# Mixture-of-experts tokens: an indexed scatter into expert slots, with four tiles loaded at a time, in place of an indexed gather for each tile

## The chip, the cores and the metric

The kernel runs on one core of one Trainium2 chip. A time is the device time of one execution in microseconds (us). Engines are named as the profile names them: PE (TensorE matmul, with PEld for its weight loads), DVE (VectorE), ACT (ScalarE), POOL (GpSimd) and SP (SyncE, which here only issues transfers). A "q" behind a name (SPq) is the engine's sequencer, which issues transfers and waits.

## The reference

The input `x` is 8 sequences of 512 tokens with 128 features, all float32. Three blocks follow one another, each with a residual: a mixture of experts, a state-space block, and the same mixture of experts again with the same weights.

```python
x = x + 0.5 * ffn(layernorm(x))        # m = 0
x = x + attn(layernorm(x))             # "ssm" below; works on one sequence at a time
x = x + 0.5 * ffn(layernorm(x))        # m = 1

def ffn(x):                            # E = 12 experts, K = 3 per token, D = 128, H = 512
    topw, sel = top_k(x @ Wg, 3); topw = softmax(topw)
    y[e] = gelu(x @ Wup[e] + bup[e]) @ Wdown[e] + bdown[e]
    return sum over the 3 chosen experts of topw * y[e]

def attn(x):
    u = silu(x @ Wg + bg) * (x @ Wi + bi)
    y = Cp * (causal convolution of u with Bp * A**t) + Dp * u
    y = layernorm(y) * gamma + beta
    return (silu(y @ Wfg + bfg) * (y @ Wfu + bfu) @ Wfd + bfd) @ Wo + bo
```

## The kernel before, in words

**Groups, slots, tiles, quads.** The sequences form three groups, `GROUPS = [[0, 1, 2], [3, 4, 5], [6, 7]]`. A group has 12 chunks of 128 tokens (the last has 8), so 36 pairs of chunk and choice (the last has 24). `route(m, g)` normalises the group's tokens into `xn`, computes the logits, takes the top three experts and gives every pair of token and choice a slot, sorted by expert and padded to whole tiles of 128 slots. `posu` (L433) holds the slot of each pair, `etab` (L484) the expert of each tile. A group has 48 tiles (the last 36), and four tiles are a quad: 12, 12 and 9 quads a group, 66 quads in both layers. Below, m0g1 is group 1 in the first layer, m1g0 group 0 in the second, and sequences carry their numbers 0 to 7.

**From slots to tokens.** A tile needs the inverse: which token sits in each slot. L439 to L472 build it on DVE and PE. In batches of 12 pairs, two one-hot tensors `M` (L447, L453) and `L` (L458) are made on DVE and multiplied on PE (L467, 12 matmuls a batch) into `ix_ps`; L472 casts it to `slot`. `xn` is also stored to DRAM (`xn_d`, L305). Then each tile is fetched by one indirect DMA on POOL (L513, through `gather_next` at L681), which reads 128 rows of `xn_d` at the indices `slot[:, t]`.

**A quad on the engines.** `prepare` transposes its four tiles on PE (L715), copies them to `xT` on ACT (L717) and loads the experts' offsets. `stage` copies the expert's up weights to `wst` on DVE (L732, one copy a tile). `up` does the first matmuls (L739) and the Gelu on ACT (L743), `down` the second (L753). After the fourth tile DVE adds the bias into `ysb` (L764) and SP stores 256 KB to `y_d` (L765).

**Back to the tokens.** When a group's last quad is stored, `finish_group` starts a `combine` for each of its sequences. For each chunk it issues three indirect gathers on POOL from `y_d` at the slots `posu` (L513, through L547), and later adds the three rows with their weights to `X` on DVE (L534). In layer 0 the sequence then goes through `ssm_block`, and when a group's sequences are all done `route(1, g)` follows; in layer 1 the sequence is stored.

**The order of the work.** Each engine executes in the order in which Python emits the instructions (`manual_schedule`, L85). The main loop (L790 to L802) walks over the 264 tiles; `up` of tile t, `down` of tile t - 2 and the staging of tiles ahead are written in turn, and twice a tile `chains.tick()` advances the generators (routes, combines, ssm blocks) by one step of a clock that counts 1.05 us a tick. POOL has its own count, `pool["free"]`, of 1.25 us for each indirect DMA (`GATHER`), and an add is emitted 3 us (`LANDS`) after its gathers by that count. `gather_upto` fetches up to 12 tiles ahead (`AHEAD`); `need` ticks on, without tile work, while the next quad's route isn't done.

Of the kernel before, what the change touches and what calls it, by code (L numbers as in the profile page):

```python
# [9 lines left out]
F32 = mybir.dt.float32  # L10
F16 = mybir.dt.float16
I32 = mybir.dt.int32
U32 = mybir.dt.uint32
# [38 lines left out]
def kernel(ctx: ExitStack, tc: tile.TileContext, a: dict, out: bass.AP):  # L52
# [9 lines left out]

    nc = tc.nc
    x = a["L0_attn_x"]
    B, T, D = x.shape
    E, _, H = a["L0_ffn_Wup"].shape
    P = 128
# [12 lines left out]
    LANDS = 3.0  # L82
    assert D == P and T == 512 and sorted(sum(GROUPS, [])) == list(range(B))

    ctx.enter_context(tc.manual_schedule())  # L85
    const = ctx.enter_context(tc.tile_pool(name="const", bufs=1))
    rt = ctx.enter_context(tc.tile_pool(name="rt", bufs=1))
    res_p = ctx.enter_context(tc.tile_pool(name="res", bufs=G + 1))
# [1 line left out]
    work = ctx.enter_context(tc.tile_pool(name="work", bufs=2))  # L90
    mo = ctx.enter_context(tc.tile_pool(name="mo", bufs=3))
    dr = ctx.enter_context(tc.tile_pool(name="dr", bufs=G + 1, space=DRAM))
    ps_up = ctx.enter_context(tc.tile_pool(name="ps_up", bufs=2, space=PSUM))
    ps_t = ctx.enter_context(tc.tile_pool(name="ps_t", bufs=1, space=PSUM))
    ps_y = ctx.enter_context(tc.tile_pool(name="ps_y", bufs=2, space=PSUM))
# [4 lines left out]
    def side_psum(shape, name):  # L100
        return ps_s.tile(shape, F32, tag="side", name=name)
# [56 lines left out]
        nc.sync.dma_start(w[n], a[f"L0_attn_{n}"])  # L158
    bo_bc = const.tile([P, D], F32, name="bo_bc")
    nc.sync.dma_start(bo_bc, a["L0_attn_bo"].unsqueeze(0).to_broadcast([P, D]))  # L160

    ones = const.tile([P, P], F16, name="ones")
    nc.vector.memset(ones, 1.0)
# [102 lines left out]
    def route(m, g, first=False):  # L266
# [5 lines left out]
        NTP = NQS[g] * 4  # L272
        chunks = [X[c][:, i, :] for c in seqs for i in range(CS)]
        r, nmr = yield from ln_stats(chunks, 1e-5, f"m{j}")
        xn = rt.tile([P, NCM, D], F32, tag="xn", name=f"xn{j}")
        xn_d = dr.tile([NC * P, D], F32, tag=f"xn_d{NC}", name=f"xn_d{j}")
        lg_ps = None
        pts: dict = {}
        xnTs: dict = {}
# [18 lines left out]
        for s in range(n):  # L298
            for i in range(CS):
                norm(  # L300
                    xn[:, s * CS + i, :], chunks[s * CS + i], r, nmr, s * CS + i,
                    not first or i % 2 == 1,
                )
            eng = nc.scalar if first else nc.sync
            eng.dma_start(  # L305
                xn_d[s * T : (s + 1) * T, :].rearrange("(p n) d -> p n d", p=P),
                xn[:, s * CS : (s + 1) * CS, :],
            )
            yield 2
        lg_ps = side_psum([P, NC, E], f"lg_ps{j}")  # L310
        for s in range(n + 1):
# [123 lines left out]
            posu.rearrange("p k c -> p (k c)"), lane, 4.0, row, op0=ALU.mult, op1=ALU.add  # L435
        )
        yield

        ix_ps = side_psum([P, NTP], f"ix_ps{j}")  # L439
        tok = mid("tok", lambda c, t: (K, c))  # L440
        nc.vector.tensor_copy(tok, tokid[:, :, :NC])
        tok = tok.rearrange("p k c -> p (k c)")
        NB_ = 12
        for b in range(NCK // NB_):
            sl = slice(b * NB_, (b + 1) * NB_)
            M = mid("M", lambda c, t: (NB_, t), F16, 2)
            nc.vector.tensor_tensor(  # L447
                M,
                iota_t[:, :NTP].unsqueeze(1).to_broadcast([P, NB_, NTP]),
                tl[:, sl].unsqueeze(2).to_broadcast([P, NB_, NTP]),  # L450
                ALU.is_equal,
            )
            nc.vector.tensor_mul(  # L453
                M, M, tok[:, sl].unsqueeze(2).to_broadcast([P, NB_, NTP])
            )
            yield
            L = rt.tile([P, NB_, P], F16, tag="L", name=f"L{j}_{b}", bufs=2)
            nc.vector.tensor_tensor(  # L458
                L,
                iota_l.unsqueeze(1).to_broadcast([P, NB_, P]),  # L460
                lane[:, sl].unsqueeze(2).to_broadcast([P, NB_, P]),
                ALU.is_equal,
            )
            yield 2
            for i in range(NB_):
                n_ = b * NB_ + i
                nc.tensor.matmul(  # L467
                    ix_ps, L[:, i, :], M[:, i, :], start=n_ == 0, stop=n_ == NCK - 1
                )
            yield  # L470
        slot = res_p.tile([P, NTP], U32, tag=f"slot{NTP}", name=f"slot{j}")
        nc.vector.tensor_copy(slot, ix_ps)  # L472

        after = mid("after", lambda c, t: (t, E))
        nc.vector.tensor_tensor(
# [6 lines left out]
        nc.vector.tensor_reduce(et, after, AX.X, ALU.add)  # L482
        etab = res_p.tile([P, NTP], I32, tag=f"etab{NTP}", name=f"etab{j}")
        nc.vector.tensor_scalar(etab, et, float(E - 1), float(WW), op0=ALU.min, op1=ALU.mult)  # L484
        y_d = dr.tile([NTP * P, D], F32, tag=f"y_d{NTP}", name=f"y_d{j}")
        cw = res_p.tile([P, K, NC], F32, tag=f"cw{NC}", name=f"cw{j}")
        res[(m, g)] = (xn_d, slot, etab, posu, cw, y_d)
        yield

        den = mid("den", lambda c, t: (K, c))  # L490
# [18 lines left out]

    pool = {"free": 0.0}  # L510

    def indirect(dst, src, idx):
        nc.gpsimd.indirect_dma_start(  # L513
            out=dst,
            out_offset=None,
            in_=src[:, :],
            in_offset=bass.IndirectOffsetOnAxis(ap=idx, axis=0),
        )
        pool["free"] = max(pool["free"], chains.now) + GATHER
        return pool["free"] + LANDS  # L520

    def combine(m, g, s, after=None):

        _, _, _, posu, cw, y_d = res[(m, g)]
        xs = X[GROUPS[g][s]]
        yg = work.tile([P, CS, K, D], F32, tag="yg", name=f"yg{m}{g}{s}", bufs=2)
        lands = []
        done = 0

        def add():  # L530
            nonlocal done
            c = s * CS + done
            for k in range(K):
                nc.vector.scalar_tensor_tensor(  # L534
                    xs[:, done, :], yg[:, done, k, :], cw[:, k, c : c + 1], xs[:, done, :],
                    op0=ALU.mult, op1=ALU.add,
                )
            done += 1

        for i in range(CS):  # L540
            for k in range(K):
                while pool["free"] > chains.now + 3 * GATHER:
                    yield
                    if done < len(lands) and lands[done] <= chains.now:
                        add()
                c = s * CS + i
                t = indirect(yg[:, i, k, :], y_d, posu[:, k, c : c + 1])  # L547
            lands.append(t)
            yield
        if after is not None:  # L550
            after()
        while done < CS:
            if lands[done] <= chains.now:
                add()
            yield
# [123 lines left out]
    state = {"gathered": 0}  # L679

    def gather_next():  # L681
        n = state["gathered"]
        p, t = tiles[n]
        m, g = phases[p]
        q = n // 4
        if n % 4 == 0:
            xg[q] = mo.tile([P, 4, D], F32, tag="xg", name=f"xg{q}", bufs=AHEAD // 4 + 1)
        xn_d, slot = res[(m, g)][:2]
        indirect(xg[q][:, n % 4, :], xn_d, slot[:, t : t + 1])
        state["gathered"] += 1  # L690

    def gather_upto(n, most):
        for _ in range(most):
            if state["gathered"] < min(n, len(tiles)) and phases[tiles[state["gathered"]][0]] in res:
                gather_next()

    def need(n):

# [6 lines left out]
    def prepare(q):  # L705

        if q >= len(quads):
            return
        need(q * 4 + 3)
        p, lq = quads[q]  # L710
        etab = res[phases[p]][2]
        pt = ps_t.tile([P, 4, P], F32, tag="t", name=f"t{q}")
        src = xg.pop(q)
        for i in range(4):
            nc.tensor.transpose(pt[:, i, :], src[:, i, :], ident)  # L715
        xT = mo.tile([P, 4, P], F32, tag="xT", name=f"xT{q}", bufs=2)
        nc.scalar.copy(xT, pt)  # L717
        xgT[q] = xT
        _, vals = nc.values_load_multi_w_load_instructions(
            etab[0:1, lq * 4 : lq * 4 + 4],  # L720
            engines=[mybir.EngineType.PE, mybir.EngineType.DVE],
            min_val=0,
            max_val=(E - 1) * WW,
            skip_runtime_bounds_check_because="min(expert, E - 1) * WW by construction",
        )
        off[q] = vals
        wst[q] = mo.tile([P, 4, WS], F32, tag="wst", name=f"wst{q}", bufs=2)
# [20 lines left out]
    def down(t, h):  # L748
        q, i = divmod(t, 4)
        if i == 0:  # L750
            y_ps[q] = ps_y.tile([P, 4, D], F32, tag="y", name=f"y{q}")
        for k in range(KH):
            nc.tensor.matmul(  # L753
                y_ps[q][:, i, :],
                h[:, k, :],
                W[:, bass.ds(off[q][i] + (WS + k * D), D)],
                start=k == 0,
                stop=k == KH - 1,
            )
        if i == 3:  # L760
            p, lq = quads[q]
            y_d = res[phases[p]][5]
            ysb = mo.tile([P, 4, D], F32, tag="ysb", name=f"ysb{q}", bufs=2)
            nc.vector.tensor_tensor(ysb, y_ps.pop(q), wst[q][:, :, H + KH : WS], ALU.add)  # L764
            nc.sync.dma_start(  # L765
                y_d[lq * 4 * P : (lq + 1) * 4 * P, :].rearrange("(p n) d -> p n d", p=P), ysb
            )
            if lq == NQS[phases[p][1]] - 1:
                finish_group(*phases[p])
# [65 lines left out]
```

## Time and profile before

| | |
|---|---|
| median of 3 runs | 801.06 us (799.05 to 802.33) |
| the profiled execution's own time | 801.01 us |
| its span, first to last instruction | 799.2 us (1.8 us lie around it) |
| busy in the span | PE 624.4, PEld 585.2, DVE 495.1, POOL 475.3, ACT 427.2 us |
| indirect DMAs on POOL | 264 for tiles (`xg`), 192 for results (`yg`) |
| moved by DMA | 64.23 MB, 80 GB/s on average |

A row of the profile's table of groups names the line, engine and operation, then `out<-in` with buffer numbers left out, then the count; behind the bar stand the busy time in us and the mean ns of one, and then the engine's idle time just before these instructions with what ended it. The first `xT` copy of a phase marks where its tiles begin: m0g0 at 67.2, m0g1 at 173.0, m0g2 at 285.8, m1g0 at 438.4, m1g1 at 565.4 and m1g2 at 673.8 us.

### The profile page before, as it was taken

To read this page: it belongs to the slowest core of one execution; us is meant where nothing else is said; L and a number is where in the kernel's file an instruction comes from. 1 tells how busy PE (TensorE), PEld (TensorE's weight loads), DVE (VectorE), ACT (ScalarE), POOL (GpSimd) and SP (SyncE) were. 2 spreads that over 40 slices of the span, in tenths; PEclk is the share of its full clock that TensorE was granted. 3 is DMA by queue.
4 is the path that set the end of the run, shared out by engine and by line. 5 is a ranking of instruction groups with operands and counts; after the bars stand their busy time and mean duration, and the time that the engine had idled before them with its cause. 6 is when DMAs were issued, how large, how long until landed. Compare 5 with 4: busy or idle time off the path is not lost.

```text
span 799.2 us, 16191 instructions
## 1 busy us (share of the span) xinstructions
PE 624.4 (78%) x5114; PEld 585.2 (73%) x5114; DVE 495.1 (62%) x1518; ACT 427.2 (53%) x1324; POOL 475.3 (59%) x479
## 2 busy tenths in 40 slices
PE   0416989999899999989334998889999989998500
PEld 0306988999888989878112998878989889998500
DVE  1486387445876666676897474987575874533422
ACT  0203854767477676767313685457677556665300
POOL 4007744435777777774003777745177777777775
PEclk9999998999999999999566999899999999999855
DMA  8801322312223322332000232322123233324322
GB/s 276 247 0 49 119 60 47 74 53 91 71 79 87 81 74 77 77 85 95 0 1 17 66 119 78 70 56 66 37 80 116 77 71 103 103 81 90 105 66 68
DMA packets 45016, 64.23 MB, mean 80 GB/s; under 512 B 9547, under 2 KB 26374, under 8 KB 44934
## 3 DMA queue, kind: packets, MB, share of 16 engines
q0 software_dynamic: 15552, 33.06, 17.6%
q1 hardware_dynamic: 28864, 29.31, 10.9%
q8 instruction: 45, 0.74, 0.4%
q10 hardware_dynamic: 518, 0.82, 0.3%
q14 instruction: 37, 0.30, 0.1%
HBM read 39.55 MB, written 23.59 MB: 79 GB/s over the span
## 4 chain that ended last, share of the span: by engine, by line
PE 44%; DVE 23%; POOL 12%; issue 10%; DMA 6%; ACT 3%; DVEq 0%; POOLq 0%; SPq 0%; ACTq 0%
PE y L753 17%; PE up L739 16%; POOL yg L513 8%; POOL xg L513 5%; DVE wst L732 3%; DVE L L458 3%; DMA xg<-xn_d,slot 3%; PE t L715 2%; DVE X L534 2%; DMA W<-in_L_ffn_Wdown_dram 2%; DVE ysb L764 1%; DMA yg<-y_d,posu 1%; PE lg_ps L293 1%; PE ing_ps L575 1%; PE fu_ps L583 1%
## 5 line engine op out<-in xcount | busy, mean ns | idle before, releaser
L513 POOL DMA_INDIRECT xg<-xn_d,slot x264 | 273.6, 1036 | 226.5 <-DVE slot L472 114.7
L743 ACT ACTIVATE h<-up,wst 128x128 f32<-128x128 f32 x1056 | 302.6, 372 | 176.9 <-ACT h L743 68.3
L739 PE MATMUL up<-xT,wst 128*128 128x128 f32 x2112 | 287.7, 280 | 1.2 <-ACT xT L717 0.7
L753 PE MATMUL y<-W,h 128*128 x2112 | 287.2, 280 | 0.0
L739 PEld LDWEIGHTS up<-xT,wst 128*128 128x128 f32 x2112 | 266.3, 197 | 9.9 <-issue 8.5
L753 PEld LDWEIGHTS y<-W,h 128*128 128x128 f32 x2112 | 264.5, 196 | 4.8 <-issue 4.8
L513 POOL DMA_INDIRECT yg<-y_d,posu x192 | 193.5, 1008 | 88.5 <-issue 82.7
L732 DVE COPY wst<-W 128x644 f32 x264 | 123.5, 508 | 7.8 <-DMA xg<-xn_d,slot 1.2
L764 DVE TENSOR_TENSOR ysb<-y,wst 128x512 f32<-128x512 f32 x66 | 45.5, 689 | 120.4 <-PE y L753 120.1
L534 DVE SCALAR_TENSOR_TENSOR X<-yg,cw,X 128x128 f32<-128x128 f32 x192 | 67.6, 352 | 64.9 <-DMA yg<-y_d,posu 61.7
L717 ACT COPY xT<-t 128x512 f32<-128x512 f32 x66 | 39.1, 593 | 55.1 <-PE t L715 49.9
L715 PE MATMUL t<-ident,xg 128*128 128x128 f32 x264 | 44.2, 286 | 14.8 <-DMA xg<-xn_d,slot 14.7
L715 PEld LDWEIGHTS t<-ident,xg 128*128 128x128 f32 x264 | 32.8, 147 | 18.3 <-DMA xg<-xn_d,slot 18.3
L467 PE MATMUL ix_ps<-M,L 128*128 128x48 f16 (+1 forms) x192 | 8.6, 194 | 37.7 <-DVE L L458 35.8
L467 PEld LDWEIGHTS <-L 128*128 128x128 f16 x192 | 7.3, 104 | 41.3 <-DVE L L458 39.9
L256 ACT ACTIVATE xn<-X,nmr_m,r_m 128x128 f32<-128x128 f32 x58 | 24.2, 501 | 24.0 <-DVE nmr_m L250 22.9
L458 DVE TENSOR_TENSOR L<-iota_l,lane 128x1536 f16<-128x1536 f16 x16 | 28.0, 1750 | 0.0
L256 ACT ACTIVATE xa<-X,nmr_a,r_a 128x128 f32<-128x128 f32 x32 | 13.2, 482 | 17.2 <-DVE nmr_a L250 17.2
L256 ACT ACTIVATE yn<-y_ps,nmr_b,r_b 128x128 f32<-128x128 f32 x32 | 12.1, 468 | 15.5 <-DVE nmr_b L250 15.5
L293 PEld LDWEIGHTS lg_ps<-wgate,xnT 128*128 128x128 f32 x128 | 17.9, 218 | 2.1 <-ACT xnT L288 2.1
L293 PE MATMUL lg_ps<-wgate,xnT 128*128 128x12 f32 x128 | 17.7, 271 | 1.8 <-ACT xnT L288 1.8
L370 PE MATMUL rk_ps<-mask,ones 128*128 128x144 f16 (+1 forms) x6 | 1.6, 263 | 21.8 <-DVE d L366 21.8
(161 smaller groups left out, 459.2 us busy)
## 6 DMA issues: line engine op xcount, KB each, us to landing
y_d<-ysb SPq DMA_DIRECT2D x66, 256.0 KB
xg<-xn_d,slot POOLq DMA_INDIRECT x264, 2.9
xn_d<-xn SPq DMA_DIRECT2D x13, 256.0 KB
W<-in_L_ffn_Wup_dram POOLq DMA_DIRECT2D x12, 256.0 KB, 7.1
W<-in_L_ffn_Wdown_dram SPq DMA_DIRECT2D x12, 256.0 KB
yg<-y_d,posu POOLq DMA_INDIRECT x192, 2.5
X<-in_L_attn_x_dram SPq DMA_DIRECT2D x8, 256.0 KB
out_dram<-X SPq DMA_DIRECT2D x8, 256.0 KB
```

What stands on the lines that cost most here:

```text
L256: nc.scalar.activation(dst, src, AF.Identity, scale=r[:, i : i + 1], bias=nmr[:, i : i + 1])
L293: nc.tensor.matmul(lg_ps[:, s * CS + i, :], xnT[:, i, :], wgate, start=True, stop=True)
L458: nc.vector.tensor_tensor(L, iota_l.unsqueeze(1).to_broadcast([P, NB_, P]), lane[:, sl].unsqueeze(2).to_broadcast([P, NB_, P]), ALU.is_equal,)
L513: nc.gpsimd.indirect_dma_start(out=dst, out_offset=None, in_=src[:, :], in_offset=bass.IndirectOffsetOnAxis(ap=idx, axis=0),)
L534: nc.vector.scalar_tensor_tensor(xs[:, done, :], yg[:, done, k, :], cw[:, k, c : c + 1], xs[:, done, :], op0=ALU.mult, op1=ALU.add,)
L715: nc.tensor.transpose(pt[:, i, :], src[:, i, :], ident)
L717: nc.scalar.copy(xT, pt)
L732: nc.vector.tensor_copy(wst[q][:, i, :], W[:, bass.ds(off[q][i], WS)])
L739: nc.tensor.matmul(pu[:, k, :], wst[q][:, i, ts(k, P)], xgT[q][:, i, :], start=True, stop=True)
L743: nc.scalar.activation(h[:, k, :], pu[:, k, :], AF.Gelu, bias=wst[q][:, i, H + k : H + k + 1])
L753: nc.tensor.matmul(y_ps[q][:, i, :], h[:, k, :], W[:, bass.ds(off[q][i] + (WS + k * D), D)], start=k == 0, stop=k == KH - 1,)
L764: nc.vector.tensor_tensor(ysb, y_ps.pop(q), wst[q][:, :, H + KH : WS], ALU.add)
```

## The change

For all groups but m0g0 (the first) the inverse index isn't built. Instead each of the 36 (or 24) pairs of chunk and choice is one indirect DMA on POOL that writes the 128 rows `xn[:, c, :]` to the slots `posu[:, k, c]` of a DRAM tensor `xs_d[g]`, which lies in slot order. A quad is then one plain 256 KB load that SP issues, and it waits for all of the group's scatters. The group counts as routed (`res`) only once its last scatter is emitted. Slots that no token fills are read too, so the three `xs_d` are set to zero at the start by three stores. `xn` gets two buffers, and `yg` becomes a tile per chunk, with six of them, where it was a tile per sequence, with two. POOL leaves the manual schedule: its order is the tile framework's own, bound by the dependencies of the data and by the "written order" links between neighbours; the built program shows scatters ahead of gathers that were written before them.

```diff
-    ctx.enter_context(tc.manual_schedule())
+    ctx.enter_context(tc.manual_schedule(engines={ET.PE, ET.DVE, ET.Activation, ET.SP}))
...
+    zero = work.tile([P, 4 * D], F32, tag="row", name="zero", bufs=4)
+    nc.vector.memset(zero, 0.0)
+    for g in range(G):
+        xs_d.append(dr1.tile([NQS[g] * 4 * P, D], F32, name=f"xs_d{g}"))
+        nc.sync.dma_start(
+            xs_d[g].rearrange("(q p n) d -> p q (n d)", p=P, n=4),
+            zero.unsqueeze(1).to_broadcast([P, NQS[g], 4 * D]),
+        )
...
-        xn = rt.tile([P, NCM, D], F32, tag="xn", name=f"xn{j}")
+        xn = rt.tile([P, NCM, D], F32, tag="xn", name=f"xn{j}", bufs=2)
...
-            eng = nc.scalar if first else nc.sync
-            eng.dma_start( xn_d ... xn ...)
+            if first:
+                nc.scalar.dma_start( xn_d ... xn ...)
...
+        if first:
             (the index build, L439 to L472, as before)
+            out_.update(xn_d=xn_d, slot=slot)
+        else:
+            chains.start(scatter(m, g, xn, posu, out_))
...
+    def queued(made):
+        ins = getattr(made, "ins", made)
+        if "last" in pool:
+            tc.add_manual_dep(ins, pool["last"].name, ORDER, reason="written order")
+        pool["last"] = ins
+        pool["free"] = max(pool["free"], chains.now) + GATHER
+        return ins
...
+    def scatter(m, g, xn, posu, out_):
+        made: list = []
+        for c in range(NCS[g]):
+            for k in range(K):
+                while pool["free"] > chains.now + 3 * GATHER:
+                    yield
+                ins = queued(
+                    nc.gpsimd.indirect_dma_start(
+                        out=xs_d[g][:, :],
+                        out_offset=bass.IndirectOffsetOnAxis(ap=posu[:, k, c : c + 1], axis=0),
+                        in_=xn[:, c, :],
+                        in_offset=None,
+                    )
+                )
+                for o in made:
+                    tc.declare_no_dep(ins, o, query=..., reason="pairs have different slots")
+                made.append(ins)
+        out_.update(scatters=made, ready=pool["free"] + LANDS)
+        res[(m, g)] = out_
+        yield
...
-        yg = work.tile([P, CS, K, D], F32, tag="yg", name=f"yg{m}{g}{s}", bufs=2)
+            yg.append(work.tile([P, K, D], F32, tag="yg", name=f"yg{m}{g}{s}_{i}", bufs=6))
...
     def gather_next():
...
+        if "slot" in r:
+            indirect(xg[q][:, n % 4, :], r["xn_d"], r["slot"][:, t : t + 1])
+            state["gathered"] += 1
+            return
+        made = nc.sync.dma_start(
+            xg[q], xs_d[g][t * P : (t + 4) * P, :].rearrange("(p n) d -> p n d", p=P)
+        )
+        for o in r["scatters"]:
+            tc.add_manual_dep(getattr(made, "ins", made), o.name, SYNC, reason="scattered rows")
+        state["gathered"] += 4
```

`gather_upto` also stops where a route's scatters have not landed by the count (`ready`).

## The prediction

> **What bounds the kernel now.** I read the windows view first, cut where each group's first `xT` copy stands. Columns: engine busy time (instructions), granted clock, DMA share, GB/s.
>
> ```profile
> core 0: us, PE busy (x) PEld busy (x) DVE busy (x) ACT busy (x) POOL busy (x), PEclk, DMA share, GB/s
> 173.00:285.80 112.80, 107.34 (x904) 101.62 (x903) 80.49 (x254) 76.07 (x239) 78.56 (x75) 0.98 0.28 77
> 285.80:366.80 81.00, 76.46 (x604) 69.98 (x603) 56.67 (x199) 57.65 (x176) 62.09 (x63) 0.98 0.31 83
> 366.80:438.40 71.60, 33.93 (x187) 22.07 (x187) 58.74 (x196) 23.63 (x56) 10.50 (x10) 0.69 0.06 20
> 438.40:565.40 127.00, 116.99 (x950) 111.30 (x951) 86.38 (x261) 77.32 (x242) 84.98 (x83) 0.93 0.27 73
> 754.10:799.20 45.10, 0.00 (x0) 0.00 (x0) 12.39 (x35) 0.00 (x0) 29.89 (x32) 0.50 0.25 72
> ```
>
> In the tile phases PE is busy 92 to 95% of the time, so they are PE-bound. Two stretches are not: the hand-over to layer 1 (366.8 to 438.4), where PE does 34 us of work in 72, and the tail after the last quad, where only POOL works. Then the groups of instructions and the waits:
>
> ```profile
> L513 POOL DMA_INDIRECT xg<-xn_d,slot x264 | 273.6, 1036 | 226.5 <-DVE slot L472 114.7
> L513 POOL DMA_INDIRECT yg<-y_d,posu x192 | 193.5, 1008 | 88.5 <-issue 82.7
> L458 DVE TENSOR_TENSOR L<-iota_l,lane 128x1536 f16<-128x1536 f16 x16 | 28.0, 1750 | 0.0
> L467 PE MATMUL ix_ps<-M,L 128*128 128x48 f16 (+1 forms) x192 | 8.6, 194 | 37.7 <-DVE L L458 35.8
> ```
>
> POOL waits long for `slot`, once for 58.7 us (the hand-over). The timeline gives the prices of a hand-over and of a bare quad:
>
> ```profile
> 180.10 0.69 DVE L764 TENSOR_TENSOR ysb<-y,wst 128x512 f32<-128x512 f32 x1 [0.38 <-PE y L753]
> 180.82 0.32 SPq L765 DMA_DIRECT2D y_d<-ysb  x1
> ...
> 184.68 0.95 POOL L513 DMA_INDIRECT yg<-y_d,posu  x1 [14.09 <-issue]
> 185.93 0.95 POOL L513 DMA_INDIRECT yg<-y_d,posu  x1 [0.30 <-issue]
> 658.66 0.59 ACT L717 COPY xT<-t 128x512 f32<-128x512 f32 x1
> 666.25 0.59 ACT L717 COPY xT<-t 128x512 f32<-128x512 f32 x1
> 673.83 0.59 ACT L717 COPY xT<-t 128x512 f32<-128x512 f32 x1
> ```
>
> A 256 KB store to DRAM is usable 3.9 us after its issue; back-to-back gathers start 1.25 us apart (0.95 busy, 0.30 issue), and with the slower ones among them I take 1.27; a quad with no side work takes 7.6 us. From the groups, an ssm block costs PE 9.2 us (transposes 10.7 + 5.4 + 10.1, matmuls 10.2 + 9.0 + 9.5 + 10.1 + 8.5, over 8).
>
> **What the Trainium skill says.** "DMA: Bandwidth & Descriptors", § SWDGE vs HWDGE vs iDMA: a DMA issued by GpSimd gets a pair of descriptors (read, write) per operation. A scatter of 128 rows then has as many as a gather, hence the same price; the trace has gathers only. Same page, § Anatomy of one DMA: most of about 2 us of fixed cost is the write receipt, heaviest when DRAM is written. Gathers land 2.4 to 5.3 us after issue here (median 2.9 for `xg`), into SBUF; for a scatter no row exists. "SBUF — State Buffer", § Who interferes with whom: GpSimd blocks while DVE runs a copy in a two-port mode. The trace agrees weakly: minimum 941 ns, mean 1036 for `xg`.
>
> **The change, part by part.**
>
> *Index build, five routes.* Removed: 13 of 16 batches, DVE 13 × (1.750 + 0.725 + 0.711) = 41 us and PE 156 × 0.045 = 7 us, 13 SP stores and 216 `xg` gathers (274 us of POOL). POOL and DVE are not the limit in the tile phases, so most of this is worth nothing by itself.
>
> *Added:* 156 scatters × 1.27 = 198 us of POOL, 54 SP loads, three zero stores of 33 × 256 KB = 8.65 MB. At the SP queue's rate (29.31 MB in 10.9% of 799.2 us, 336 GB/s) these take 26 us from 36 us on. The DMA engines are idle then until the first gathers at 59.6, so 1 us is charged (0 to 5).
>
> *m0g0 to m0g1: +16.* `posu` is ready at 117.4. In the built program 15 `xg` gathers and the 36 scatters then share POOL: 51 × 1.27 = 65 us, to 182.4. Landing 2.6 (between the medians of `yg`, 2.5, and `xg`, 2.9) and a load 3.9 bring the first `xT` to 189, where it was at 173. PE stands in order behind that transpose with half a quad and m0g1 queued, and the store of m0g0's last quad stands behind the load on SP; before, the gathers were 25 us ahead. Bounds +10 and +30 (scatter at 1.15 and 1.55).
>
> *m0g1: 112.8 becomes 134.* POOL no longer mixes `xg` with `yg`: the results of m0g0 come back in 36 gathers without `xg` between, so ssm 0 to 2 all fall in m0g1, where about 1.5 did: + 1.5 × 9.2 - 1 for the index matmuls = + 13. And the order costs a wait: in POOL's order 22 of m0g2's 24 scatters stand ahead of or among the gathers of sequence 2, while DVE's fixed order has their adds where the count put them. The add of the sequence's third chunk is reached about 64 us into the phase, its rows land at 12 + 24 × 1.25 + 19 scatters × 1.25 + 9 × 1.25 + 2.4, about 79. DVE is held 15 us; PE has staged weights for about 7 us of it. + 8. m0g2 begins at 323 (was 285.8).
>
> *m0g2 and the hand-over: 152.6 becomes 117.* Work: 9 × 7.6 = 68.4, ssm 3, 4 and half of 5 (2.45 × 9.2 = 22.5), route 6, some inefficiency 2: 99. Then the rest of ssm 5 runs alone, a chain of DVE, PE and ACT steps of 15 (bounds 15 and 30: in the crowded hand-over of before the last block took 30), and a wait for adds of 3 as above. POOL is done by then: 12 + 72 × 1.25 + 2.4 + 3.9 = 108. The 58.7 us wait for `slot` goes because the route runs under m0g2's tiles; what is late next is ssm 5. m1g0 begins at 440 (was 438.4), with a block and a half more done.
>
> *m1g0: 127 becomes 121.* 91.2 + two blocks 18.3 + routes 9.4 + a cool clock 2. The 36 scatters come after all `yg` here and end 15 us early. m1g1 begins at 561 (was 565.4).
>
> *m1g1: 108.4 becomes 110.* Bare 91.2 + 4. But 14 scatters stand ahead of the eighth chunk's gathers, and 8 ahead of the eleventh's. The eighth chunk's rows land at 12 + 31.5 + 17.5 + 2.4 = 63, the add is reached at 45: 18 us held, about 10 for PE; the eleventh adds some 5. m1g2 begins at 671.
>
> *m1g2 and tail: 125.4 becomes 116.* No `xg` on POOL: eight quads at 7.6 and 15 to the last `ysb` are 76 (was 80.3). The last 24 gathers no longer queue behind those of m1g1: 0.7 + 3.9 + 24 × 1.24 + the 5.8 from the last gather's end to the span's end give 40 (was 45.1).
>
> Sum of the span: 189 + 134 + 117 + 121 + 110 + 76 + 40 = 787; with the 1.8 us around it **789 us**. The profiled execution took 801.01, the median is 801.06, so no correction.
>
> **Rivals.**
> 1. *The scatter's price (slower).* Some 100 POOL operations stand in a row with the end (36 before m0g1, 19 and 22 before held adds in m0g1 and m1g1, 22 in m0g2). Each 0.1 us more per scatter costs about 10 us; from 1.39 on the gain is gone. At 1.6: 0.33 × 100 = 33, **822 us**. For it: receipts from DRAM, and that no row shows it. Against: equal descriptor counts.
> 2. *Held adds cost PE nothing (faster).* If staged weights and the scatters' placing cover them, 8 + 3 + 15 = 26 come off: **763 us**. Against: m1g1 is PE-bound and recovers nothing.
> 3. *Gains and waits cancel:* 801. A scatter price between 1.35 and 1.43 does it.
> 4. *The order isn't as built:* not likely, since the program's lists show 156 scatters and 54 loads.
>
> **How the numbers follow.** No change means within 0.5% (4 us), about what a measurement can tell. As worked out 0.43, rival 2 0.14, so faster 0.57; rival 3 0.12; rival 1 0.31. The range reaches from rival 2's end to rival 1's, 762 to 824; the likeliest case's own is 775 to 797.
>
> **What would show it.** First `xT` of m0g1 near 189 with POOL full before it; the hand-over's wait for `slot` gone; DVE waits `X<-yg` above the 61.7 us of before, in m0g1 and m1g1; a scatter row near 1.0 us; last `ysb` near 747 and 40 us behind it. It is wrong if scatters have a mean above 1.2, if m1g0 doesn't begin within 10 us of 440, or if PE is held before m1g2 for another reason.

## The result and the profile after

The changed kernel took 843.01 us (median of 4 runs, 837.93 to 845.45) against 800.63 for the kernel before: a ratio of 1.0521 (95% interval [1.0466, 1.0575]; brackets behind a ratio mean this below), slower by 42 us, where 789 us were predicted. Its profiled execution has a span of 836.2 us. The experiments ran on several chips, and three of them are slower for every kernel (before itself: 1028 to 1051 us), so the text gives ratios to the kernel before on the same chip, and compares lengths of phases only between chips on which that kernel takes 798 to 801.

The page's groups of the changed kernel (`xs_d` is the scatter):

```profile
L549 POOL DMA_INDIRECT yg<-y_d,posu x192 | 191.0, 995 | 285.3 <-DMA xg<-xs_d 174.3
L817 PE MATMUL up<-xT,wst 128*128 128x128 f32 x2112 | 293.7, 284 | 35.1 <-DVE wst L810 31.5
L566 POOL DMA_INDIRECT xs_d<-xn,posu x156 | 160.1, 1026 | 69.6 <-issue 37.8
L597 DVE SCALAR_TENSOR_TENSOR X<-yg,cw,X 128x128 f32<-128x128 f32 x192 | 67.4, 352 | 102.5 <-DMA yg<-y_d,posu 99.6
```

The wait for `slot` is gone and a scatter is priced like a gather (1026 and 995 ns). Two waits are new or larger: DVE's adds `X` wait 99.6 us for gathered rows, and PE's `up` waits 31.5 us for staged weights. In the kernel before, `up` waited 1.2 us in all, and the adds 61.7 for rows:

```profile
L534 DVE SCALAR_TENSOR_TENSOR X<-yg,cw,X 128x128 f32<-128x128 f32 x192 | 67.6, 352 | 64.9 <-DMA yg<-y_d,posu 61.7
```

The windows view, cut as before at each group's first `xT`, here m0g1, m0g2 with the hand-over, m1g0 and m1g1:

```profile
core 0: us, PE busy (x) PEld busy (x) DVE busy (x) ACT busy (x) POOL busy (x), PEclk, DMA share, GB/s
188.30:333.60 145.30, 124.30 (x928) 111.88 (x928) 91.31 (x320) 85.76 (x261) 61.77 (x60) 0.91 0.23 70
333.60:462.70 129.10, 104.09 (x736) 89.38 (x735) 88.29 (x304) 72.69 (x214) 73.42 (x72) 0.92 0.23 72
462.70:598.60 135.90, 119.74 (x936) 111.80 (x936) 88.46 (x309) 84.95 (x260) 61.38 (x60) 0.95 0.25 79
598.60:719.80 121.20, 95.46 (x821) 94.86 (x821) 51.15 (x141) 62.19 (x206) 59.48 (x60) 0.89 0.30 92
```

In the kernel before, m1g1 was the line

```profile
565.40:673.80 108.40, 102.70 (x897) 98.61 (x896) 72.39 (x224) 72.50 (x230) 74.38 (x72) 1.00 0.30 83
```

m0g2 with the hand-over is shorter, 129.1 us where it was 152.6, and PE is idle in it for 25.0 us where it was for 42.2. But m0g1, m1g0 and m1g1, in which PE was 92 to 95% busy, are longer, with PE 79 to 88% busy. In m1g1 the waits and the timelines of POOL, DVE and PE show where the time goes:

```profile
DVE X L597 <- DMA yg<-y_d,posu: 42.5, 17, 17.7
PE up L817 <- DVE wst L810: 25.0, 2, 15.2
```

```profile
655.77 0.96 POOL L566 DMA_INDIRECT xs_d<-xn,posu  x1 [0.30 <-issue]
657.03 0.98 POOL L549 DMA_INDIRECT yg<-y_d,posu  x1 [0.30 <-DMA xs_d<-xn,posu]
```

```profile
659.53 0.39 DVE L597 SCALAR_TENSOR_TENSOR X<-yg,cw,X 128x128 f32<-128x128 f32 x1 [17.67 <-DMA yg<-y_d,posu]
```

```profile
663.92 2.05 PE L817 MATMUL up<-xT,wst 128*128 128x128 f32 x8 [15.20 <-DVE wst L810]
```

The scatter at 655.77 is the last of 14 in a row that stand ahead of the gather at 657.03. The row of that gather lands at 659.5; until then DVE has stood in its fixed order for 17.67 us, with the copies of the next quad's weights behind the add, and PE stands for 15.20 behind those.

### The profile page after: what moved, and what is told of

The parts are those of the page before. It is cut to its first block, busy times and chain, and to the rows that moved or that the text cites. A ratio compares the mean times of both kernels' runs of the same rounds, so it can differ in the third digit from the quotient of the medians.

```text
span 836.2 us, 15919 instructions
## 1 busy us (share of the span) xinstructions
PE 627.1 (75%) x4958; PEld 586.1 (70%) x4958; DVE 452.0 (54%) x1470; ACT 425.5 (51%) x1324; POOL 407.9 (49%) x419
## 3 DMA queue, kind: packets, MB, share of 16 engines
q1 hardware_dynamic: 39040, 48.71, 17.6%
## 4 chain that ended last, share of the span: by engine, by line
PE 40%; DVE 21%; POOL 13%; issue 11%; DMA 10%; ACT 3%; SPq 1%; DVEq 0%; POOLq 0%; ACTq 0%
PE y L831 15%; PE up L817 15%; POOL yg L549 7%; POOL xs_d L566 5%; DMA yg<-y_d,posu 3%; DVE wst L810 3%; DMA xs_d<-xn,posu 2%; DVE X L597 2%; DMA W<-in_L_ffn_Wdown_dram 2%; PE t L793 2%; PE lg_ps L307 2%; DVE ysb L842 2%; DMA xg<-xn_d,slot 1%; POOL xg L549 1%; PE ing_ps L639 1%
## 5 line engine op out<-in xcount | busy, mean ns | idle before, releaser
L549 POOL DMA_INDIRECT yg<-y_d,posu x192 | 191.0, 995 | 285.3 <-DMA xg<-xs_d 174.3
L817 PE MATMUL up<-xT,wst 128*128 128x128 f32 x2112 | 293.7, 284 | 35.1 <-DVE wst L810 31.5
L817 PEld LDWEIGHTS up<-xT,wst 128*128 128x128 f32 x2112 | 271.5, 200 | 47.2 <-issue 41.2
L566 POOL DMA_INDIRECT xs_d<-xn,posu x156 | 160.1, 1026 | 69.6 <-issue 37.8
L597 DVE SCALAR_TENSOR_TENSOR X<-yg,cw,X 128x128 f32<-128x128 f32 x192 | 67.4, 352 | 102.5 <-DMA yg<-y_d,posu 99.6
L549 POOL DMA_INDIRECT xg<-xn_d,slot x48 | 48.7, 1014 | 61.9 <-DVE slot L490 47.6
L793 PE MATMUL t<-ident,xg 128*128 128x128 f32 x264 | 43.1, 282 | 31.5 <-DMA xg<-xs_d 20.1
L633 PE MATMUL yn_ps<-ident,yn 128*128 128x128 f32 x32 | 10.6, 359 | 15.4 <-ACT yn L270 14.9
L633 PE MATMUL xa_ps<-ident,xa 128*128 128x128 f32 x32 | 10.8, 366 | 11.5 <-ACT xa L270 10.8
L633 PEld LDWEIGHTS yn_ps<-ident,yn 128*128 128x128 f32 x32 | 4.7, 148 | 20.8 <-ACT yn L270 20.8
```

Source lines behind the costliest of these rows:

```text
L549: nc.gpsimd.indirect_dma_start(out=dst, out_offset=None, in_=src[:, :], in_offset=bass.IndirectOffsetOnAxis(ap=idx, axis=0),)
L566: nc.gpsimd.indirect_dma_start(out=xs_d[g][:, :], out_offset=bass.IndirectOffsetOnAxis(ap=posu[:, k, c : c + 1], axis=0), in_=xn[:, c, :], ...
L597: nc.vector.scalar_tensor_tensor(xs[:, done, :], yg[done][:, k, :], cw[:, k, c : c + 1], xs[:, done, :], op0=ALU.mult, op1=ALU.add,)
L817: nc.tensor.matmul(pu[:, k, :], wst[q][:, i, ts(k, P)], xgT[q][:, i, :], start=True, stop=True)
```

## Experiments

Two theories. **A:** the loss is POOL's order, in which scatters overtake gathers that were written before them, so adds are held. **B:** 156 scatters themselves cost too much, by POOL's time in series or by what they do to others.

### 1. The scatters in written order

```diff
+        if scattered and "gather" in pool and pool["gather"] is not pool["last"]:
+            tc.add_manual_dep(ins, pool["gather"].name, ORDER, reason="behind the gathers")
+        if not scattered:
+            pool["gather"] = ins
```

> The change with one more link: a scatter may not stand ahead of a gather that was written before it, so POOL runs xg, then all yg of a group, then the next group's scatters; nothing else differs. Theory A (scatters put ahead of the gathers hold the adds on DVE, and with them the weights of PE and the late steps of the ssm blocks): the long holds of X<-yg at 270 and 640 to 690 us vanish, the m1g1 phase falls from 121 to 95-100, m0g1 from 145 to 128-135, the hand-over phase from 129 to 120-125; device time near 803 (793 to 812). Theory B (a tile waits for a whole group's scatters, which is what costs): m0g1 still begins at 188, and the time falls by at most 10, to 833 or more.

> The change, with each scatter linked behind the last gather that was written before it, so that no scatter overtakes a yg gather and no add is held behind one. If the held adds carry most of the loss (my theory by the prediction: some 20 us), the ratio falls from 1.052 to 1.03 or less where the matmuls issue freely; if they are a symptom of POOL being full, 1.04 to 1.05. Twice before on chips with a lower granted clock it was 0.011 under the change.

> The change with its scatters in written order (behind the gathers written before them), again, as the control of the three runs beside it, whose POOL instructions stand in this order. Three times before: 1.064 to 1.072 of the kernel before.

Measured: on the three slower chips 1.0723 [1.0646, 1.08], 1.0681 [1.0609, 1.0753] and 1.0644 [1.0571, 1.0717]; on a chip where the kernel before takes 798.94, **1.0012 [1.0001, 1.0023]** (799.89 us). There POOL's order was the whole loss against the kernel before. The windows of that run, m0g1 to m1g1, and its wait for rows in m1g1:

```profile
188.10:321.20 133.10, 121.56 (x928) 109.91 (x928) 92.03 (x320) 85.90 (x260) 61.32 (x60) 0.96 0.25 77
321.20:450.40 129.20, 104.12 (x738) 89.41 (x737) 88.58 (x304) 72.75 (x215) 73.54 (x72) 0.92 0.23 72
450.40:586.10 135.70, 119.55 (x936) 111.64 (x935) 88.32 (x309) 84.91 (x260) 61.22 (x60) 0.95 0.25 79
586.10:681.30 95.20, 91.72 (x818) 90.94 (x817) 52.83 (x145) 62.18 (x206) 60.40 (x60) 1.00 0.38 117
```

```profile
DVE X L602 <- DMA yg<-y_d,posu: 15.0, 17, 1.8
```

Against the change, m0g1 is 12.2 us shorter and m1g1 26.0. No run of the change is on record for this chip; that its phases can be set beside these follows from the other phases, which agree within 0.3 us. PE's wait for staged weights in m1g1 falls from 25.0 us to 0.9. On the one slower chip that ran both orders (the 1.0681), the change took 1.0799: there undoing the order gave about 1%, and the intervals overlap. Part 4 comes back to those chips.

### 2. What the 156 scatters cost

On the same chip, three edits of the change itself. In the traces of d1 and d2 POOL's operations stand in the order of the run above, one for one, though without the added link:

```diff
 (d1: a gather of as many rows into an unread SBUF tile; SP loads zeros; xn has one buffer)
-                        out=xs_d[g][:, :],
-                        out_offset=bass.IndirectOffsetOnAxis(ap=posu[:, k, c : c + 1], axis=0),
-                        in_=xn[:, c, :],
+                        out=seen[:, (c * K + k) % NCM, :],
+                        in_=xs_d[g][:, :],
+                        in_offset=bass.IndirectOffsetOnAxis(ap=posu[:, k, c : c + 1], axis=0),
 (d2: a plain transfer to rows in a row)
+                    nc.gpsimd.dma_start(out=xs_d[g][n * P : (n + 1) * P, :], in_=xn[:, c, :])
 (d3: nothing issued; only the count goes on)
+                pool["free"] = max(pool["free"], chains.now) + GATHER
```

These expectations were written for a chip on which the written order takes 1.06 to 1.07. The runs fell on one on which it takes 1.0012, and are read against that.

> Each scatter replaced, in its place, by a gather of the same size: 128 rows of 512 B taken from the zeroed DRAM tensor at the same positions into an SBUF tile that nothing reads; the SP loads still wait for the whole group of them, and read zeros. POOL's instructions are as many and about as long (0.96 us). If it is POOL's time in series and the wait for the whole group, 1.06 to 1.07 as the control. If it is the scatter itself (rows written to DRAM in an order of their own, behind which others' transfers or instruction fetches stand), 1.01 to 1.03, with PE idle in some 20 to 30% of these windows as in the gathers' and not 65 to 70%.

> Each scatter replaced, in its place, by a POOL transfer without an index: the same 128 rows of 512 B written to 128 rows in a row of the same DRAM tensor (wrong slots). If writing 64 KB from POOL's software queue is what costs, 1.05 to 1.07; if the index and its descriptors cost, 1.01 or less.

> The scatters left out altogether; the written order's clock goes on as if they were there, and SP loads zeros. It is the floor of what all 156 scatters together cost: if they carry the whole loss and more, 0.93 to 0.97, as two thirds of them gave 1.01 to 1.02 against 1.07; if something else of the change costs too (SP's loads, the zeroing, the earlier ssm blocks), above 1.00.

Measured: gathers in the scatters' places 0.9999 [0.9984, 1.0014], plain writes 0.9747 [0.9715, 0.9779], none 0.9673 [0.9644, 0.9703]. POOL's groups of the first two:

```profile
L567 POOL DMA_INDIRECT seen<-xs_d,posu x156 | 155.9, 999 | 69.1 <-issue 46.3 <-DVE posu L448 13.7 <-DVE msum_a L247 8.5
```

```profile
L567 POOL DMA_DIRECT2D xs_d<-xn x156 | 86.5, 563 | 0.4 <-issue 0.4
```

So writing to DRAM by index costs the end no more than reading by index, and most of the cost is the index's time on POOL: 1.0 us busy and 0.3 of issue, against 0.56 and no gap for a plain write. (A plain write also doesn't wait for `posu`: the first starts at 102.0 instead of 115.7. That head start was not needed: m0g1 begins at 168.4, at 168.1 with no scatter at all, and 36 × 0.56 + 15 gathers × 1.27 = 39 us from 115.7 on would also have been in time, by an estimate from these prices.) All scatters together are worth 797.4 - 769.3 = 28 us of span. 20.0 of these lie ahead of m0g1, whose first quad waits for all 36 (188.1 against 168.1 without); most of the rest is 1.7 in m1g0, 3.0 in m1g1 and 2.6 in the tail. The floor of 0.967 is also the most that free scatters could bring in this kernel: 798.9 - 772.3 = 27 us. The windows without scatters, m0g1 to m1g0:

```profile
168.10:301.00 132.90, 121.60 (x929) 109.97 (x930) 93.72 (x327) 85.89 (x261) 37.66 (x36) 0.96 0.21 65
301.00:429.80 128.80, 104.17 (x736) 89.57 (x735) 87.33 (x304) 72.67 (x214) 35.87 (x36) 0.92 0.18 54
429.80:563.80 134.00, 118.74 (x937) 111.08 (x936) 87.85 (x309) 84.86 (x260) 23.30 (x24) 0.95 0.20 62
```

Lengths are as with scatters, within 1.7 us. PE is idle 11.3 + 24.6 + 15.3 = 51 us in them; in the kernel before it was 5.5 + 42.2 + 10.0 = 58 over the same three phases. The hole of the hand-over was for the most part not filled, it was spread: PE's waits in m0g2 here are `yn_ps` for ACT's `yn` (8.3 us), `xa_ps` (4.1), `y_ps` (3.9) and `rk_ps` (2.5), which are steps of the ssm blocks and the route.

Leaving out only the third choice's scatters (104 instead of 156, so a third of the slots stays zero), in the change's own order, on two slower chips:

```diff
-            for k in range(K):
+            for k in range(K - 1):
```

> The change with the third choice's scatters left out (104 scatters instead of 156; the slots of the third choice keep zeros, so that part of the result is left out), all else as it is. Theory P (POOL's time for scatters, some 100 operations in a row with the end): 33 to 42 us come off, near 805; m0g1 begins near 173. Theory A: more in the places where scatters stand ahead of gathers, m1g1 near 105 and m0g1 near 135, and the total near 800. If the loss lies elsewhere (work moved on PE, the loads on SP): m0g1 begins earlier and the rest of the phases stay, about 828.

> The change without the third choice's scatters (104 instead of 156; those slots keep zeros, which leaves that part of the result out). Theory P, some 100 POOL operations in a row with the end: 33 to 42 less than the change, near 805, m0g1 from 173. If the phases after m0g1's start stay as they are: 828. At the lower clock it was at 1.019 of before, against 1.072 for the written order with all scatters: there the scatters' number counted most.

Measured 1.0189 [1.0116, 1.0262] and 1.0099 [1.0059, 1.0138]. On the second of these chips the whole change is 1.0799: 75 us for 52 scatters, or 1.4 us each. There undoing the order of all of them gives about 14 us, and on the faster chip all 156 are worth 28. Part 4 takes that up.

### 3. The first hand-over without scatters

The index build and gathers for m0g1 as well as m0g0 (`by_gather = first or (m, g) in ((0, 1),)` in place of `first`), in the change's order and in written order:

> The change, but m0g1 too is fetched by the index build and a gather for each tile, as before; the other four groups are scattered. Theory B: m0g1 begins at 173 instead of 188, and about 15 us come off: 828. If the scatters' place ahead of the gathers also cost in m0g1 (theory A), xg and yg now share POOL there and the order is another one: up to 10 more come off or are lost, 818 to 838.

> Both of the former: written order on POOL and m0g1 by gathers. Theory A with B: the two gains add up, near 788 (778 to 800), below the kernel before. If the only cost was the wait for whole groups (B alone): 825. m0g1 begins at 173; POOL carries 36 xg, 36 yg and 24 scatters in m0g1, some 122 us at 1.27, so its ssm blocks come later and the hand-over may give back up to 10.

> Scatters in written order, and the second group (m0g1) by index build and gathers as the kernel before has it. On the chip where the written order alone took 1.001, the scatters' own cost of 28 us lay in the first hand-over for 20: m0g1's first tile waited for 36 scatters to end, 188.1 against 168.1 without them, and 173.0 with the kernel before's gathers. With gathers there it should start at 173 and all that follows keep its lengths (133, 129, 136, 95, 75, 41): 782 us, a ratio of 0.98. On a chip where engines' issue is slow beside POOL's runs it should repeat 1.06.

Measured on a slower chip 1.0668 [1.0606, 1.0729] and, with written order, 1.0624 [1.0562, 1.0687]; on a chip with the kernel before at 798.2, **1.005 [1.0034, 1.0066]**, not the 0.98 expected. The windows of that run, m0g1 and m0g2:

```profile
170.90:307.90 137.00, 117.16 (x912) 105.51 (x912) 96.47 (x334) 83.65 (x253) 92.64 (x92) 0.93 0.26 72
307.90:452.50 144.60, 114.84 (x753) 98.20 (x752) 90.72 (x320) 76.12 (x222) 73.12 (x72) 0.88 0.22 66
```

m0g1 does start at 170.9, 17 us earlier. But its tile gathers now share POOL with the 36 gathers of m0g0's results, which run from 182.3 to 271.2 instead of 203.3 to 250.3; the 24 scatters of m0g2 end at 302.6 instead of 282.6; and m0g2 begins at 307.9, 39 us after the last quad of m0g1. m1g0 begins at 452.5, where it began at 450.4: in both runs 17.7 us after the `state` of ssm 5 (434.8 and 432.7), so it was that chain, not the scatters, that set it; without any scatter the distance is the same (412.2 to 429.9). The 17 us were given back within two phases.

### 4. Scatters in the second layer only, and other chips

One group alone, m1g0, scattered (`by_gather = (m, g) != (1, 0)`), and the whole second layer (`by_gather = m == 0`):

> The kernel before with one group, the first of the second layer (m1g0), scattered and loaded by SP; the other five keep the index build and the gathers, and only one DRAM tensor is zeroed. If the loss of the change comes from scatters that stand beside full work (held adds, a group that can't start before its 36th scatter), and the gain at the hand-over is the scatter's own, m0g1, m0g2, m1g1 and m1g2 take what they took before (106, 113, 127, 108 us by first xT) and the hand-over shortens by 20 to 25 us, as 152.6 fell to 129.1 with the whole change: a ratio of about 0.97. If the hand-over's gain came from work that the other groups had lost (their index builds), it does not appear and the ratio is 1.00. If 36 scatters in a row cost about what the index build cost, also 1.00.

> Gathers and index builds for all of the first layer, scatters for all three groups of the second. Against the run with m1g0 alone it adds the scatters of m1g1 and m1g2: with the whole change m1g1 took 27 us more and m1g2's phase and its hand-over 6 to 7 us less, so theory one (scatters cost where they stand beside full work) says a ratio of 0.99 to 1.00, 0.02 above the run with m1g0 alone; if the scatters cost only by holding adds that other scatters' order puts off, about the same, since m1g1's 18 and 10 us of held adds are here too; if only m0g1's start and m0g2 were to blame, 0.97.

> Only m1g0 scattered. Where issue was slow it took 0.988: the hand-over itself became longer (posu to the first xT 67 us for 36 scatters in a row and SP's load, against 31 for index build and gathers), and m1g1 shorter by 20. On the faster chip the hand-over costs the same 30 to 36 us more, since nothing hides 36 times 1.28 us there, and less is to be won from m1g1 (108 us before, 95 at best): 1.01 to 1.02. If the hand-over there is as short as with the whole change (129 us), 0.97.

Measured on a slower chip 0.988 [0.9825, 0.9936] and 1.0196 [1.0141, 1.0251], the second above all that was expected; m1g0 alone on the faster chip **1.0365 [1.0344, 1.0385]**, about twice the expected loss. So no version that computes the whole result was found that beats the kernel before on the faster chips; m1g0 alone is 1.2% below it on a slower one. The last run's windows up to and over the hand-over:

```profile
282.40:364.00 81.60, 77.13 (x601) 70.63 (x601) 56.35 (x198) 57.67 (x176) 62.71 (x63) 0.96 0.31 77
364.00:458.20 94.20, 41.12 (x185) 25.75 (x185) 63.53 (x246) 30.42 (x71) 39.31 (x40) 0.69 0.13 43
```

The hole grows from 71.6 to 94.2 us, which is 22.6 of the 23.9 us between the two profiled executions (823.1 and 799.2). `posu` is ready at 404.6, the 36 scatters run from 405.6 to 452.5, and the first `xT` stands at 458.2: 53.6 us from `posu`, where index build and first gathers took 30.7 (407.7 to 438.4). In this bare stretch the index build is the shorter way. In the whole change `posu` is ready at 373.5, under m0g2's tiles, and the scatters of m1g0 end 22 us ahead of its first `xT`, so the hand-over does not wait for them.

The remaining runs on the slower chips are the change again, the written order, both edits of part 3, and the kernel before for its trace:

> The change itself, as the control of this set: the first set ran where PE was granted a clock of 0.80 to 0.85 and the kernel before took 1028 us, so nothing there can be set beside the 843 of the change. At a clock as in the prediction's trace: 843 (838 to 846). At the lower clock: a ratio to before of 1.06 to 1.09.

> The change with POOL in the written order (scatters behind the gathers written before them). Theory A (scatters ahead of gathers hold the adds on DVE and, behind them, PE): at full clock 803 (793 to 812), m1g1 95 to 100 instead of 121, m0g1 128 to 135 instead of 145. Theory B (the wait for a whole group's scatters alone): 833 or more. Rival C (the cost is PE's own: matmuls of the ssm blocks stand in PE's order where the count put them and wait for their chains whatever POOL does): m1g1 falls, having no ssm block, m0g1 and the hand-over phase stay within 5 of 145 and 129, the total near 818.

> Written order on POOL and m0g1 fetched by gathers. A with B: 788 (778 to 800) at full clock. C: PE's waits in the ssm blocks stay, near 805. At the lower clock the ratio to the kernel before was 1.062 where the written order alone had 1.072, so there the gathers for m0g1 gave 1% and no more is expected of them.

> The kernel before itself, for its trace beside these: whether gaps in which PE issues nothing though nothing is awaited also stand in its runs of xg and yg gathers. If any indirect DMA on POOL slows the other engines' issue, its gathers (264 xg, 192 yg) show as much of it per instruction as the scatters do; if it is the scatters, PE's issue gaps are some 50 us at most here against 190 with the change.

Measured: the change 1.0799 [1.0726, 1.0871], both edits 1.0607 [1.0546, 1.0668]. The windows of the written order on such a chip (the one of the 1.0681), a run of scatters, a stretch with POOL idle, a run of gathers; then PE within the scatters:

```profile
883.10:912.10 29.00, 5.98 (x18) 4.48 (x18) 1.67 (x5) 1.73 (x5) 22.27 (x23) 0.52 0.20 64
922.00:978.00 56.00, 56.00 (x504) 56.00 (x503) 22.81 (x52) 37.87 (x124) 0.00 (x0) 1.00 0.24 79
978.70:1008.90 30.20, 12.57 (x83) 11.08 (x82) 4.34 (x11) 4.61 (x16) 23.14 (x24) 0.69 0.25 68
```

```profile
898.32 0.37 PE L836 MATMUL y<-W,h 128*128 x1 [1.73 <-issue]
899.72 0.57 PE L836 MATMUL y<-W,h 128*128 x1 [1.03 <-issue]
901.13 0.37 PE L836 MATMUL y<-W,h 128*128 x1 [0.84 <-issue]
903.24 0.37 PE L836 MATMUL y<-W,h 128*128 x1 [1.73 <-issue]
```

The same scatters in the same order on the faster chip:

```profile
646.30:676.20 29.90, 28.95 (x260) 28.75 (x260) 11.25 (x24) 19.50 (x64) 23.18 (x23) 1.00 0.35 114
```

There PE does 260 matmuls in 30 us, here 18: it gets one every 1.4 to 2.1 us and waits for nothing that the profile shows. Such gaps of PE, over 0.3 us long and without a recorded wait, were laid over POOL's runs of transfers: on the slower chips they fill 49 to 58% of the time of the scatters (change and written order), 22 to 32% of that of the `yg` gathers there, and 14% (`xg`) and 20% (`yg`) in the kernel before. On the faster chips there are none. On the chip that ran both, these gaps sum to 212.5 us in the written order and 118.4 in the kernel before, 94 more, where the run is 69 us longer. So the loss that written order leaves on the slower chips is of about this size; and with a third of the scatters left out, on the second slower chip, the gaps over them fall from 98 to 33 us. What holds the engines' issue, and why a scatter does so more than a gather, no run shows.

## Why the prediction was wrong

Point by point, with the change's phases and those of the run in written order.

- **The start, m0g0 to m0g1, was right, in part by luck.** 189 was predicted, 188.3 measured. `posu` was ready at 115.0 and not at 117.4; the 51 POOL operations took 67.3 us and not 65; and a scatter's landing and SP's load, 2.2 and 2.9 us where 2.6 and 3.9 were taken, made up for the rest. The zero stores show no cost: m0g0 began at 66.5, before at 67.2.
- **The scatter's price (rival 1) was right in the forecast's favour.** 1026 ns is the row; gathers in the scatters' places take as long. No extra time for writing DRAM shows either: a scatter lands in 2.2 us, a gather into SBUF in 2.6. The slower result did not come from that rival.
- **Held adds: the mechanism was right, its size was not.** The terms were 8 in m0g1, 3 in m0g2 and 15 in m1g1. Undoing the order gave 12.2, 0 and 26.0: 38 instead of 26. The failing step is how much of a hold reaches PE. In m1g1, at the eighth chunk, DVE was held 17.7 us where 18 was expected, and PE ran on for 6.9 of them on staged weights (641.9 to 648.7), near the 7 to 8 that were taken. But the end of DVE's wait does not release PE: two more late rows, a bias add and the copy of the weights come first, 4.4 us (659.5 to 663.9), for which the sum had no term. So PE was idle for 15.2 us instead of "about 10". At the eleventh chunk DVE was held 9.9 us, of which staged weights covered 3.8, and 3.6 came on top: 9.8 instead of "some 5". In m0g1 DVE was held for 11.3 us at once, not 15; still PE's waits grew, by 4.7 for weights and by 5.8 for an ssm step of DVE (`y_ps`), which the term left out. Rival 2, that the holds cost nothing, is refuted for m1g1.
- **m0g1, m0g2 and m1g0 without holds: the larger error.** The sum had 126, 114 and 121 us; the written order has 133.1, 129.2 and 135.7, together 37 more, and they are as long with no scatter at all. The work was about right (m0g1: PE busy + 14.2 where + 13 was charged; m1g0: 119.6 where 120.9 was). What failed is that ssm blocks among tiles were charged as PE's work alone ("+ 1.5 × 9.2", "two blocks 18.3"): no idle time came with them beyond the 5.5 us that m0g1 had before and 2 for "a cool clock" in m1g0. PE is idle 11.5 us in m0g1 and 16.2 in m1g0; in m0g2 it is 25.1, where 15 for the rest of ssm 5 was allowed. PE's waits without any scatter, in m0g1 and m1g0, and then m1g0 of the kernel before (at the end of a row: us in all, times, the longest):

```profile
PE yn_ps L618 <- ACT yn L270: 4.2, 2, 2.7
PE xa_ps L618 <- ACT xa L270: 2.3, 1, 2.3
PE y_ps L618 <- DVE y L659: 1.5, 1, 1.5
```

```profile
PE xa_ps L618 <- ACT xa L270: 4.3, 1, 4.3
PE t L778 <- DMA xg<-xs_d: 4.0, 1, 4.0
PE rk_ps L384 <- DVE d L380: 3.3, 1, 3.3
PE y_ps L618 <- DVE y L659: 1.5, 1, 1.5
PE yn_ps L618 <- ACT yn L270: 1.5, 1, 1.5
```

```profile
PE ix_ps L467 <- DVE L L458: 5.8, 2, 3.4
PE rk_ps L370 <- DVE d L366: 3.8, 1, 3.8
```

`xa_ps`, `yn_ps` and `y_ps` are PE's steps of an ssm block, for whose inputs it waits in its order; before they cost 0.9 us in m0g1 and 0.4 in m1g0. The 4.0 us in m1g0 are of another kind: SP issues the second quad's load only behind a store. The kernel with m1g0 alone scattered agrees: there m0g1, with the ssm blocks where they were before, is 112.0 us, and m1g0, in which both blocks of sequences 6 and 7 then run (before, the second ran in m1g1), 135.2. No run moved the ssm blocks alone, so that these waits make up the error is read from the traces, not shown by an edit. For the last chain of ssm 5, at the end of m0g2, 15 was near: 17.6 (`state` at 445.1, first `xT` at 462.7).
- **"What is late next is ssm 5" was right, its worth was not.** 35.6 us were to come from m0g2 and the hand-over; 23.5 came, and m0g1 and m1g0 gave back 20.3 and 8.7 without any hold. m1g0 began at 462.7, so the sign that the prediction named, more than 10 us from 440, came.
- **m1g1 without its hold, m1g2 and the tail were right.** 95, 76 and 40 predicted; 95.2, 74.6 and 41.5 measured.

The holds are 12 short and the phases without them 37: together the 49 us by which the span missed (836.2 against 787).

## What to carry to other kernels

When an edit takes one engine out of a written order, read that engine's built order against the orders that stay fixed: an add that waits for an overtaken gather holds everything behind it, here 38 us for some forty scatters ahead of gathers in m0g1 and m1g1. An empty stretch that is filled with other chains' steps is worth only the idle time that does not come back as in-order waits elsewhere; compare PE's idle time over all phases that the work moves through, not the hole's alone. An indexed transfer costs the same time on POOL whichever way it goes, so a scatter of pairs in place of a gather of tiles can pay only where other work covers POOL's run.

## What the runs showed of the hardware

- A scatter of 128 rows of 512 B from SBUF to DRAM takes POOL 1.03 us in the mean, and in a run of them one starts every 1.27 us in the median; a gather of as many rows takes 1.00 and 1.25. A plain POOL write of the same rows takes 0.56 us.
- On three of the chips PE issues little while POOL runs indirect transfers one behind another. On one of them it was 18 matmuls in 29 us of scatters, 83 in 30 us of gathers, and 504 in 56 us with POOL idle. In no trace of the faster chips does PE have such a gap.
